# A two-layer sequence kernel: its background work ordered by an estimate of readiness, a product in column pairs, and masks moved to VectorE

## The chip, the cores and the metric

One core of a Trainium2 chip. The metric is device time of one execution in microseconds (us), the median of the runs. Engines are named TensorE (PE in the profile; PEld is its weight load), VectorE (DVE), ScalarE (ACT), GpSimd (POOL) and SyncE (SP), which issues the DMAs.

## The reference, cut to what is computed

```python
x = L0_attn_y_all                       # 4 sequences x 2048 tokens x 256
x = x + attn0(layernorm(x))             # one head, keys and values 64 wide, causal softmax
x = x + ffn0(layernorm(x))              # fp8-quantized input and weight, one 256x256 product
x = x + attn1(layernorm(x))             # 16 heads of 16, rotary positions, causal softmax
x = x + ffn1(layernorm(x))              # mix with the token before, sigmoid(r) * (relu(k)^2 @ Wv)
```

## The kernel before, in words

The work is cut into 16 chunks of 512 tokens: four sequences (b) of four chunks (qb). A chunk attends to its own and the earlier chunks of its sequence, so chunk qb has 4(qb+1) key tiles of 128.

**The main loop** is layer 1's attention. It runs over the chunks, in each over four groups of four heads (g), in each over the key tiles (kt): 640 steps. A step has

- the scores of four heads (`scores_of`, L640): for each head a product of 32 rows (16 key values and their rounding remainders) with the queries' high part, one with the low part, and one that adds the row shift; where the tile lies on the diagonal, four small bf16 products with `maskT_p` add minus infinity (L650). ScalarE takes the exponential (L657);
- the row maxima of four heads for a later group (`maxima_of`, L607): two products a head, on the diagonal four small products with `mask_p` (L615), then a VectorE maximum (L622). `all_maxima` fixes at which step each is due; near a change of chunk several fall into one step, and `whole_maxima` issues those beyond the first by themselves;
- the values of the step before (`weighted`, L680): four products of 32 columns each.

Scores and maxima use TensorE as four strips of 32 rows, so two score heads and two maxima heads share it: `together` issues pass by pass over the heads, first half of a step with score heads 0 and 1 and maxima heads 2 and 3, then the values, then the other half. The values use it as four strips of 32 columns. Every other product uses all 128 rows and columns.

**The background work** fills in between: generators of layer 0 for a chunk two or three ahead (list A: `a_in`, `a_mid`, `a_out`), layer 1's projections for the next chunk (Bq: `b_in`, `b_project`, `b_keys`, `b_queries`; Q: the second half of the queries) and the end of the chunk before (E: `end_half`). Each generator yields after a piece with its cost in us of TensorE time. At the end of every step `pull` takes pieces while the step's credit lasts. The credit is at least 1.75 us a step, more where a list must be done by a date (`rate_of`). A generator that yields a cost of 0 or more is not taken twice in one step; that, and a count of two steps in `b_keys`, is the only distance kept between a piece and what it waits for. `force` drains a list that is due.

**Layer 0** (`a_in`, `a_mid`, `a_out`): queries and keys are projected with the weights written twice, so that 128 rows hold the value twice (L327, 8 matmuls for half a chunk in the profile's records); the low parts are what rounding left (L334). `a_mid` takes the row maxima (L364, with a mask product L369 on the diagonal, maximum L370), then for each key tile the scores (L395 to L400), the exponential (L403) and the product with the values and a column of ones (L407), which adds up in one PSUM bank over the whole chunk: 65 columns, so that the row sum comes out beside the 64 values. `a_out` multiplies by the output weights (L429), whose 65th row is the bias, divides, and runs layer 0's feed-forward part.

**Buffers.** Seven PSUM banks are shared by all products, one more is layer 1's accumulator. `w2` is a pool of 13 buffers of 128 x 512; `live` counts those in use, and `full(n)` keeps two free. In each engine the program order is the order of issue. SyncE's queue has the loads, one x load a chunk (L109) and two output stores a chunk (L776).

Of the kernel before, what the change touches and what calls it, by code (L numbers as in the profile page):

```python
# [22 lines left out]
P = 128  # L23
# [11 lines left out]
NEG = -1e30  # L35


W2, PT = 13, 6
# [4 lines left out]
def seq_kernel(  # L43
# [26 lines left out]
    const = ctx.enter_context(tc.tile_pool(name="const", bufs=1))  # L70
    kv = ctx.enter_context(tc.tile_pool(name="kv", bufs=NB + 1))
# [13 lines left out]
    mask_b = const.tile([P, P], BF16, name="mask_b")  # L85
    make_causal_mask(nc, mask_b, mask_val=NEG)

# [28 lines left out]
    wqk0 = load_w(wqk0T, "wqk0", 4 * D0)  # L116
    wv0 = load_w(wv0T, "wv0", D0)
    bqk = const.tile([P, 2], F32, name="bqk")
# [4 lines left out]

    wo0 = const.tile([D0 + 1, C + 1], F32, name="wo0")
    nc.gpsimd.memset(wo0, 0.0)
    nc.gpsimd.memset(wo0[D0 : D0 + 1, C : C + 1], 1.0)
    nc.sync.dma_start(wo0[:D0, :C], wo0T)
    nc.sync.dma_start(wo0[D0 : D0 + 1, :C], bo0.rearrange("(o c) -> o c", o=1))
# [57 lines left out]
    for name, keep, fill, first, step in (  # L186
        ("ident_p", ALU.not_equal, 1.0, 1, -1),
        ("mask_p", ALU.is_ge, NEG, 1, -1),
        ("maskT_p", ALU.is_ge, NEG, -1, 1),
    ):  # L190
        t = const.tile([P, HG, P], BF16, name=name)
        nc.gpsimd.memset(t[:SLOT], 0.0)
        nc.gpsimd.affine_select(
            out=t[:SLOT], in_=t[:SLOT], pattern=[[first * SLOT, HG], [step, P]],
            compare_op=keep, fill=fill, base=0, channel_multiplier=first,
        )
        for h in range(1, HG):
            nc.sync.dma_start(t[h * SLOT : (h + 1) * SLOT], t[:SLOT])
        parts.append(t)
    ident_p, mask_p, maskT_p = parts  # L200
# [30 lines left out]
    HALF = BLK // 2  # L231

# [39 lines left out]
    def normal_T(x, out_to, hf, tag):  # L272

        my = stats(x, hf, tag)
        yield 0.0
        while full(2):
            yield None
        xn = w2n(f"xn_{tag}_{hf}")
        normalize(x, hf, my, xn)
        yield 0.0  # L280
        if not out_to:
            out_to.append(w2t(f"xT_{tag}_{hf}"))
        transpose(xn, out_to[0], f"{tag}_{hf}", nc.scalar.copy)
        done(1)
        yield 0.6
# [20 lines left out]
    def a_in(b, qb, x, hf):  # L306
# [6 lines left out]
        xT = to[0]  # L313
        if hf == 0:
            while full(2):
                yield None
            kT0[qb] = kv.tile([P, BLK], F32R, tag="kT0", name=f"kT_{tag}", bufs=NB)
            v0[qb] = kv.tile([P, TT, D0 + 1], F32, tag="v0", name=f"v_{tag}", bufs=NB)
            nc.gpsimd.memset(v0[qb][:, :, D0 : D0 + 1], 1.0)
            q0[b, qb] = w2(f"qh_{tag}", F32R), w2(f"ql_{tag}", F32R)  # L320
        kT, va, (qh, ql) = kT0[qb], v0[qb], q0[b, qb]
        flags.add((b, qb, "a", hf))
        cols = slice(hf * HALF, (hf + 1) * HALF)
        pq = bank(f"pq_{tag}_{hf}")
        for i in range(2):
            for k in range(CK):
                nc.tensor.matmul(  # L327
                    pq[:, i * HALF : (i + 1) * HALF], wqk0[:, k, i * P : (i + 1) * P],
                    xT[:, k, :], start=(k == 0), stop=(k == CK - 1),
                )  # L330
        for i, hi, lo, r in ((0, qh, ql, slice(0, P)), (1, kT, kT, slice(D0, P))):
            src = pq[:, i * HALF : (i + 1) * HALF]
            nc.scalar.activation(hi[:, cols], src, AF.Identity, bias=bqk[:, i : i + 1])
            nc.vector.scalar_tensor_tensor(  # L334
                lo[r, cols], src[r, :], bqk[r, i : i + 1], hi[r, cols].bitcast(F32),
                ALU.add, ALU.subtract,
            )
        yield -1.8
        pv = bank(f"pv_{tag}_{hf}")
        for j in range(2):  # L340
# [3 lines left out]
            va[:, 2 * hf : 2 * hf + 2, :D0],  # L344
# [4 lines left out]
        yield 0.9  # L349
        flags.add((b, qb, "in", hf))  # L350

    def a_mid(b, qb):
# [3 lines left out]
        qh, ql = q0.pop((b, qb))  # L356

        mx = small.tile([P, TT, NB], F32, tag="mx0", name=f"mx_{tag}")
        for t in range(TT):
            for kb in range(qb + 1):  # L360
                sc = bank(f"m_{tag}_{t}_{kb}")
                w = BLK if kb < qb else (t + 1) * P
                for q in (qh, ql):
                    nc.tensor.matmul(  # L364
                        sc[:, :w], q[:, t * P : (t + 1) * P], kT0[kb][:, :w],
                        start=(q is qh), stop=(kb < qb and q is ql),
                    )
                if kb == qb:
                    nc.tensor.matmul(sc[:, w - P : w], ident_b, mask_b, start=False, stop=True)  # L369
                nc.vector.reduce_max(mx[:, t, kb : kb + 1], sc[:, :w], axis=AX.X)  # L370
                if kb % 2 or kb == qb:
                    yield -0.6 * (1 + kb % 2)
# [3 lines left out]
        yield 0.0  # L376
        while full(3):
            yield None
        sh = w2(f"sh_{tag}", F32R)
        shift_rows(pads[2], sh, f"sh_{tag}")  # L380
        yield 0.5

        av = bank(f"av_{tag}")
        nkt = (qb + 1) * TT
        last = None
        for kt in range(nkt + 1):
            now = None
            if kt < nkt:
                while full(1):
                    yield None  # L390
                sc = bank(f"s_{tag}_{kt}")
                pT = w2(f"p_{tag}_{kt}")
                c0 = max(kt - qb * TT, 0) * P
                keys = kT0[kt // TT][:, (kt % TT) * P : (kt % TT + 1) * P]
                nc.tensor.matmul(sc[:, c0:], keys, qh[:, c0:], start=True, stop=False)  # L395
                nc.tensor.matmul(sc[:, c0:], keys, ql[:, c0:], start=False, stop=False)
                diag = kt >= qb * TT
                nc.tensor.matmul(sc[:, c0:], ones, sh[:, c0:], start=False, stop=not diag)
                if diag:
                    nc.tensor.matmul(  # L400
                        sc[:, c0 : c0 + P], ident_b, maskT_b, start=False, stop=True
                    )
                nc.scalar.activation(pT[:, c0:], sc[:, c0:], AF.Exp, scale=D0**-0.5)  # L403
                now = (kt, pT, c0)
            if last is not None:
                k, p, c = last
                nc.tensor.matmul(  # L407
                    av[: D0 + 1, c:], v0[k // TT][:, k % TT, :], p[:, c:],
                    start=(k == 0), stop=(k == nkt - 1),
                )  # L410
                done(1)
            last = now
            yield -1.7
        done(3)
        cx = w2(f"cx_{tag}")[: D0 + 1, :]
        nc.scalar.copy(cx, av[: D0 + 1, :])
        yield 0.0
        ctx0[b, qb] = cx

    def a_out(b, qb, x, hf):  # L420
# [4 lines left out]
        cx = ctx0[b, qb]  # L425
        t2 = slice(2 * hf, 2 * hf + 2)
        for t in range(2 * hf, 2 * hf + 2):
            o = bank(f"po_{tag}_{t}")
            nc.tensor.matmul(  # L429
                o[:, : C + 1], cx[:, t * P : (t + 1) * P], wo0, start=True, stop=True  # L430
            )
# [5 lines left out]
        if hf:  # L437
            done(1)
        my = stats(x, hf, f"f{tag}")
        yield 1.0  # L440
# [8 lines left out]
        yield 0.0  # L449
# [9 lines left out]
        yield 0.5  # L459
# [8 lines left out]
        yield 0.6  # L468
# [14 lines left out]
    def b_project(b, qb):  # L483

        tag = f"a1_{b}_{qb}"
        for t in range(TT):
            while (b, qb, t // 2) not in xT1 or full(2):
                yield None
            if t == 0:
# [25 lines left out]
            roped[b, qb, t] = count[0], qk, rb  # L515
            yield -1.8
# [8 lines left out]
            yield 0.9  # L525

    def b_keys(b, qb):

        tag = f"a1_{b}_{qb}"
        for t in range(TT):  # L530
            while (b, qb, t) not in roped or count[0] < roped[b, qb, t][0] + 2:
                yield None
            _, qk, kn = roped.pop((b, qb, t))
# [7 lines left out]
            yield 0.0  # L541
# [12 lines left out]
            yield -0.5  # L554

    def b_queries(b, qb, pair, hf):

        tag = f"a1_{b}_{qb}_{pair}"
        while (
            (b, qb, "k", 2 * hf + 1) not in flags or full(1)  # L560
            or (pair and order.index((b, qb)) > at[0] and at[1] < 2)
        ):
            yield None
        qd = w2(f"qd_{tag}_{hf}")
        src = qr1[b, qb][:, 2 * hf : 2 * hf + 2, pair * P : (pair + 1) * P]
# [6 lines left out]
        yield 0.0  # L572
# [7 lines left out]
        qh, ql = q1[b, qb, pair]  # L580
        pt = bank(f"pt_{tag}_{hf}")
# [11 lines left out]
        yield -0.5  # L593


    def maxima_of(b, qb, g, s, mx, heads):
# [3 lines left out]
        qs = [q[:, g % 2, :] for q in q1[b, qb, g // 2]]  # L600
        cols = slice(t * P, (t + 1) * P)
        w = BLK if kb < qb else (t + 1) * P
        scs = {h: bank(f"m_{b}_{qb}_{g}_{s}_{h}") for h in heads}

        def pass_(i, h):
            r = slice(h * SLOT, (h + 1) * SLOT)
            nc.tensor.matmul(  # L607
                scs[h][:, :w], qs[i][r, cols], kT1[b, kb][r, g, :w],
                start=(i == 0), stop=(kb < qb and i == 1),
            )  # L610

        def mask(v, h):
            if kb == qb:
                r = slice(h * SLOT, (h + 1) * SLOT)
                nc.tensor.matmul(  # L615
                    scs[h][:, w - P + v * SLOT : w], ident_p[r, v, :],
                    mask_p[r, v, v * SLOT :], start=False, stop=(v == HG - 1),
                )

        def drain():  # L620
            for h in heads:
                nc.vector.reduce_max(mx[:, t, h, kb : kb + 1], scs[h][:, :w], axis=AX.X)  # L622

        return heads, pass_, 2, mask, drain

    def scores_of(b, qb, g, kt, sh, heads):

        qs = [q[:, g % 2, :] for q in q1[b, qb, g // 2]]
        c0 = max(kt - qb * TT, 0) * P
        kcols = slice((kt % TT) * P, (kt % TT + 1) * P)  # L630
        diag = kt >= qb * TT
# [462 lines left out]
```

## Time and profile before

| | |
|---|---|
| runs | 3276.69, 3259.07, 3256.58 us; median 3259.07 |
| the profiled execution: its own time, its span | 3270.68 us, 3268.9 us |
| busy share: PE, PEld, DVE, ACT, POOL | 94%, 53%, 64%, 53%, 20% |
| mean granted TensorE clock | 0.955 |
| chain that ended last | PE 73%, DVE 18%, ACT 4%, issue 3%, POOL 2%, DMA 1% |
| idle time of TensorE, first matmul at | 182.5 us, 11.8 us |

The busy time of TensorE counts from a matmul's start to a modelled end, and matmuls overlap, so a busy PE is not PE at its peak. What a stretch of work costs TensorE is better read from the start of its first matmul to the start of the next stretch's first. A group's row gives instructions, busy time (overlaps counted once), mean duration of one, and the idle time of its engine just before, with what ended it. An fp32 product of 128x512 appears as two records.

### The profile page before, as it was taken

To read this page: it belongs to the slowest core of one execution; us is meant where nothing else is said; L and a number is where in the kernel's file an instruction comes from. 1 tells how busy PE (TensorE), PEld (TensorE's weight loads), DVE (VectorE), ACT (ScalarE), POOL (GpSimd) and SP (SyncE) were. 2 spreads that over 40 slices of the span, in tenths; PEclk is the share of its full clock that TensorE was granted. 3 is DMA by queue.
4 is the path that set the end of the run, shared out by engine and by line. 5 is a ranking of instruction groups with operands and counts; after the bars stand their busy time and mean duration, and the time that the engine had idled before them with its cause. 6 is when DMAs were issued, how large, how long until landed. Compare 5 with 4: busy or idle time off the path is not lost.

```text
span 3268.9 us, 75100 instructions
## 1 busy us (share of the span) xinstructions
PE 3086.4 (94%) x31392; PEld 1738.1 (53%) x31392; DVE 2080.0 (64%) x4408; ACT 1732.1 (53%) x3649; POOL 637.8 (20%) x991
## 2 busy tenths in 40 slices
PE   7889999999999999899999999989999999999988
PEld 4555555555556555545456555554545655554444
DVE  4556657676647676576745666667673677577771
ACT  2435455455555545546565454554655555555664
POOL 4312203121113301313003220122210421021000
PEclk8889899899999999989999899989999999999999
DMA  2000000000000000000000000000000000000000
GB/s 64 2 1 14 1 1 14 1 5 11 2 2 14 15 1 1 14 1 14 1 2 2 15 15 1 5 11 1 14 1 1 5 11 8 1 8 1 8 2 7
DMA packets 21045, 24.66 MB, mean 8 GB/s; under 512 B 1793, under 2 KB 20450, under 8 KB 20706
## 3 DMA queue, kind: packets, MB, share of 16 engines
q1 hardware_dynamic: 20706, 19.87, 1.9%
q8 instruction: 246, 4.03, 0.5%
q14 instruction: 93, 0.76, 0.1%
HBM read 11.18 MB, written 8.39 MB: 6 GB/s over the span
## 4 chain that ended last, share of the span: by engine, by line
PE 73%; DVE 18%; ACT 4%; issue 3%; POOL 2%; DMA 1%; POOLq 0%; ACTq 0%; DVEq 0%
PE s L640 19%; PE av L680 15%; DVE mx L622 10%; PE m L607 8%; PE av_a L407 4%; PE pq_a L267 3%; PE s L650 2%; PE pk_f L751 2%; PE po_f L267 2%; PE m_a L364 2%; PE m L615 2%; PE pr_f L267 1%; PE pw_f L267 1%; PE pv_a L267 1%; PE s_a L395 1%
## 5 line engine op out<-in xcount | busy, mean ns | idle before, releaser
L622 DVE TENSOR_REDUCE mx<-m 128x1 f32<-128x512 f32 (+3 forms) x2560 | 1423.8, 604 | 721.7 <-PE m L607 331.5
L657 ACT ACTIVATE p<-s 128x512 f32<-128x512 f32 (+3 forms) x2560 | 1224.5, 532 | 1189.7 <-PE s L640 626.7
L607 PE MATMUL m<-kT_a,qh_a 32*128 32x512 f32 (+3 forms) x2560 | 735.5, 471 | 78.8 <-DVE mx L622 41.3
L680 PE MATMUL av<-p,v_a 128*32 128x512 f32 (+3 forms) x5120 | 642.0, 560 | 0.1
L640 PE MATMUL s<-qh_a,kT_a 32*128 32x512 f32 (+3 forms) x2560 | 622.3, 466 | 15.8 <-DVE mx L622 14.0
L640 PEld LDWEIGHTS s<-qh_a,kT_a 32*128 32x128 f32 x2560 | 255.1, 186 | 705.9 <-issue 285.6
L607 PE MATMUL m<-kT_a,ql_a 32*128 32x512 f32 (+3 forms) x2560 | 561.8, 392 | 0.0
L640 PE MATMUL s<-ql_a,kT_a 32*128 32x512 f32 (+3 forms) x2560 | 510.1, 396 | 0.0
L640 PE MATMUL s<-sh,ones 32*128 32x512 f32 (+3 forms) x2560 | 478.8, 370 | 0.0
L607 PEld LDWEIGHTS m<-kT_a,qh_a 32*128 32x128 f32 x2560 | 314.8, 189 | 206.2 <-DVE mx L622 127.2
L607 PEld LDWEIGHTS m<-kT_a,ql_a 32*128 32x128 f32 x2560 | 276.4, 192 | 0.0
L640 PEld LDWEIGHTS s<-sh,ones 32*128 32x128 f32 x2560 | 248.5, 190 | 24.3 <-ACT sh L301 2.3
L640 PEld LDWEIGHTS s<-ql_a,kT_a 32*128 32x128 f32 x2560 | 246.1, 189 | 0.0
L241 POOL TENSOR_SCALAR v_f<-mv_f 128x2 f32<-128x2 f32 x32 | 7.0, 219 | 964.1 <-DVE mv_f L239 963.6
L615 PE MATMUL m<-mask_p,ident_p 32*128 32x96 bf16 (+3 forms) x4096 | 194.5, 203 | 0.0
L680 PEld LDWEIGHTS av<-p,v_a 128*32 128x32 f32 x5120 | 107.8, 109 | 156.2 <-issue 121.3
L650 PE MATMUL s<-maskT_p,ident_p 32*128 32x32 bf16 (+3 forms) x4096 | 172.5, 198 | 0.0
L407 PE MATMUL av_a<-p_a,v_a 128*65 128x512 f32 (+3 forms) x320 | 145.5, 536 | 2.8 <-ACT p_a L403 1.6
L615 PEld LDWEIGHTS <-ident_p 32*128 32x128 bf16 x4096 | 135.5, 97 | 3.8 <-issue 0.6
L267 PE MATMUL pq_a<-wqkv,xT_a 128*128 128x512 f32 x256 | 128.8, 627 | 0.0
L650 PEld LDWEIGHTS <-ident_p 32*128 32x128 bf16 x4096 | 90.0, 93 | 47.9 <-issue 35.5
L241 POOL TENSOR_SCALAR v_a<-mv_a 128x2 f32<-128x2 f32 x64 | 14.1, 221 | 461.7 <-DVE mv_a L239 460.9
(160 smaller groups left out, 3847.3 us busy)
## 6 DMA issues: line engine op xcount, KB each, us to landing
x<-in_x SPq DMA_DIRECT2D x16, 512.0 KB, 4.1
out_y<-x SPq DMA_DIRECT2D x32, 256.0 KB, 2.1
wqkv<-in_wqkv1T SPq DMA_DIRECT2D x1, 768.0 KB, 9.2
wqk<-in_wqk0T SPq DMA_DIRECT2D x1, 256.0 KB, 4.3
wc<-in_wfT SPq DMA_DIRECT2D x1, 256.0 KB, 7.6
wo<-in_wo1T SPq DMA_DIRECT2D x1, 256.0 KB, 5.1
wr<-in_wrT SPq DMA_DIRECT2D x1, 256.0 KB, 5.0
wk<-in_wkT SPq DMA_DIRECT2D x1, 256.0 KB, 5.0
```

The lines of the kernel that those rows point to most:

```text
L267: nc.tensor.matmul(dst, lhsT[:, k, t * P : (t + 1) * P], w[:, k, :], start=(k == 0), stop=(k == CK - 1),)
L364: nc.tensor.matmul(sc[:, :w], q[:, t * P : (t + 1) * P], kT0[kb][:, :w], start=(q is qh), stop=(kb < qb and q is ql),)
L395: nc.tensor.matmul(sc[:, c0:], keys, qh[:, c0:], start=True, stop=False)
L407: nc.tensor.matmul(av[: D0 + 1, c:], v0[k // TT][:, k % TT, :], p[:, c:], start=(k == 0), stop=(k == nkt - 1),)
L607: nc.tensor.matmul(scs[h][:, :w], qs[i][r, cols], kT1[b, kb][r, g, :w], start=(i == 0), stop=(kb < qb and i == 1),)
L615: nc.tensor.matmul(scs[h][:, w - P + v * SLOT : w], ident_p[r, v, :], mask_p[r, v, v * SLOT :], start=False, stop=(v == HG - 1),)
L622: nc.vector.reduce_max(mx[:, t, h, kb : kb + 1], scs[h][:, :w], axis=AX.X)
L640: nc.tensor.matmul(scs[h][:, c0:], ones[r, :] if i == 2 else kT1[b, kt // TT][r, g, kcols], sh[r, c0:] if i == 2 else qs[i][r, c0:], start ...
L650: nc.tensor.matmul(scs[h][:, c0 : c0 + (v + 1) * SLOT], ident_p[r, v, :], maskT_p[r, v, : (v + 1) * SLOT], start=False, stop=(v == HG - 1),)
L657: nc.scalar.activation(pTs[h][:, c0:], scs[h][:, c0:], AF.Exp, scale=DK**-0.5)
L680: nc.tensor.matmul(av[h * SLOT : (h + 1) * SLOT, c0:], v1[b, kt // TT][:, kt % TT, at : at + SLOT], pTs[h][:, c0:], start=(kt == 0), stop= ...
L751: nc.tensor.matmul(pk[:, d * HALF : (d + 1) * HALF], wk[:, k, d * P : (d + 1) * P], xk[:, k, :], start=(k == 0), stop=(k == CK - 1),)
```

## The change

Five edits go together.

1. **The order of the background work.** A class `Clock` follows the instructions as they are issued and keeps, with fixed costs, when each engine would be free and when each operand would be written. A generator now yields before a piece: its cost, the `w2` buffers that it needs, and the operands that it reads. `pull` takes a piece only if the latest of these is no more than 150 ns after TensorE's place on that clock; `pull_first` (in `force`, in the start-up and ahead of a chunk's `cn`) takes the one that would be ready first. The two-step count in `b_keys` and the once-a-step rule are gone. The credit is no longer at least 1.75 us a step: it is `min(1.75, spare work / steps left in the chunk)`.
2. **Layer 0's values.** `narrow_values` handles two key tiles at once: four products of 32 columns (two tiles, two halves of the 64 values) into the four strips of a fresh bank. ScalarE copies the bank out, GpSimd adds it to `cx` and adds the two exponentials to `sums`; the output weights stand twice above each other (`wo0` is 128 rows), so their product adds the two tiles' strips, and a product with a column of ones gives the row sum. The bias is added to x by GpSimd in `a_in`. A pair is taken right behind layer 1's `weighted` when its exponentials are there.
3. **Layer 0's queries and keys** are projected once (128 columns for both together), rounded once, and written twice by six DMAs a chunk on SyncE's queue.
4. **The maxima's masks** on the diagonal, in both layers, are no longer products: `row_max` has VectorE add a mask tile and take the maximum in one `tensor_tensor_reduce`.
5. `together` goes over the four heads in turn, each head's exponential or maximum issued right behind its last product; in the second half of a step the maxima heads come first. `w2` has 12 buffers.

```diff
+    def row_max(dst, sc, w, diag):
+        if diag:
+            trash = small.tile([P, BLK], BF16, tag="trash", name="trash", bufs=1)
+            nc.vector.tensor_tensor_reduce(
+                trash[:, :w], sc[:, :w], mask_w[:, BLK - w :], 1.0, LOWEST, ALU.add, ALU.max, dst
+            )
+        else:
+            nc.vector.reduce_max(dst, sc[:, :w], axis=AX.X)
...
-        pq = bank(f"pq_{tag}_{hf}")
-        for i in range(2):
-            for k in range(CK):
-                nc.tensor.matmul(
-                    pq[:, i * HALF : (i + 1) * HALF], wqk0[:, k, i * P : (i + 1) * P],
-                    xT[:, k, :], start=(k == 0), stop=(k == CK - 1),
-                )
...
+        pq = bank(f"pq_{tag}_{hf}")[:, :HALF]
+        for k in range(CK):
+            nc.tensor.matmul(pq, wqk0[:, k, :], xT[:, k, :], start=(k == 0), stop=(k == CK - 1))
...
+        if hf:
+            for dst, src in (
+                (qh[:D0], th[:D0]), (qh[D0:], th[:D0]), (kT[:D0], th[D0:]),
+                (ql[:D0], tl[:D0]), (ql[D0:], tl[:D0]), (kT[D0:], tl[D0:]),
+            ):
+                nc.sync.dma_start(dst.bitcast(F32), src.bitcast(F32))
...
-                nc.tensor.matmul(
-                    av[: D0 + 1, c:], v0[k // TT][:, k % TT, :], p[:, c:],
-                    start=(k == 0), stop=(k == nkt - 1),
-                )
...
+    def narrow_values():
+        b, qb, kt, c0, pTs, cx, sums = narrow.pop(0)
+        tag = f"a0_{b}_{qb}_{kt}"
+        av = bank(f"av_{tag}")
+        for z in range(4):
+            j, d = divmod(z, 2)
+            nc.tensor.matmul(
+                av[z * SLOT : (z + 1) * SLOT, c0:],
+                v0[kt // TT][:, kt % TT + j, d * SLOT : (d + 1) * SLOT], pTs[j][:, c0:],
+                start=True, stop=True,
+            )
+        if kt == 0:
+            nc.scalar.copy(cx, av)
+            nc.gpsimd.tensor_tensor(sums, pTs[0], pTs[1], ALU.add)
+        else:
+            part = w2(f"avs_{tag}")
+            nc.scalar.copy(part[:, c0:], av[:, c0:])
+            for add, to in ((part, cx), (pTs[0], sums), (pTs[1], sums)):
+                nc.gpsimd.tensor_tensor(to[:, c0:], to[:, c0:], add[:, c0:], ALU.add)
+            done(1)
+        done(2)
+        flags.add((b, qb, "ctx", kt))
...
-        def mask(v, h):
-            if kb == qb:
-                r = slice(h * SLOT, (h + 1) * SLOT)
-                nc.tensor.matmul(
-                    scs[h][:, w - P + v * SLOT : w], ident_p[r, v, :],
-                    mask_p[r, v, v * SLOT :], start=False, stop=(v == HG - 1),
-                )
...
+    def pull(lists, floor):
+        some, moved = False, True
+        while moved:
+            moved = False
             for gens in lists:
                 for gen in list(gens):
...
+                    t = start_of(gens, gen)
+                    if t is None or t > clock.pe + SLACK:
                         continue
...
+                    if asked[id(gen)][0] and credit <= floor:
                         continue
...
+                    emit(gens, gen)
                     moved = some = True
...
-        rate = BASE
+        spare = sum(loads[id(z)][0] for z in (A, Bq, Q, E)) + sum(
+            a_work(*order[j]) for j in range(a_next, min(i + 4, N))
+        )
+        rate = min(BASE, spare / to(4))
...
             if last is not None:
                 weighted(*last)
+                clock.follow()
+                if narrow and clock.when(*narrow[0][4]) < clock.pe + SLACK:
+                    narrow_values()
```

## The prediction

> **What bounds the kernel now.** I read the page first: the busy shares, the clock row, the chain.
>
> ```profile
> PE 3086.4 (94%) x31392; PEld 1738.1 (53%) x31392; DVE 2080.0 (64%) x4408; ACT 1732.1 (53%) x3649; POOL 637.8 (20%) x991
> ...
> PEclk8889899899999999989999899989999999999999
> ...
> PE 73%; DVE 18%; ACT 4%; issue 3%; POOL 2%; DMA 1%; POOLq 0%; ACTq 0%; DVEq 0%
> ```
>
> TensorE is the bound, VectorE the second link (18% of the chain). The clock is mostly full; at its mean of 0.955 it costs (1 - 0.955) x 3269 = 147 us. Then TensorE's timeline in one step, at full clock: is the half step with mask products longer?
>
> ```profile
> 1122.76 0.49 PE L640 MATMUL s<-qh_a,kT_a 32*128 32x512 f32 x2
> 1122.76 0.50 PE L607 MATMUL m<-kT_a,qh_a 32*128 32x512 f32 x2
> ...
> 1123.32 0.40 PE L640 MATMUL s<-sh,ones 32*128 32x512 f32 x2
> 1123.65 0.66 PE L546 MATMUL pk_a<-ident,rb_a 128*128 128x128 f32 x4
> 1124.14 1.03 PE L267 MATMUL pv_a<-wqkv,xT_a 128*128 128x256 f32 x4
> 1125.10 0.49 PE L640 MATMUL s<-qh_a,kT_a 32*128 32x512 f32 x2
> ...
> 1125.45 0.32 PE L615 MATMUL m<-mask_p,ident_p 32*128 32x128 bf16 x8
> 1125.67 0.39 PE L640 MATMUL s<-sh,ones 32*128 32x512 f32 x2
> 1125.99 0.64 PE L680 MATMUL av<-p,v_a 128*32 128x512 f32 x4
> ```
>
> It is not. The half without masks runs from 1122.76 to 1123.65, the half with eight from 1125.10 to 1125.99: both 0.89 us. The masks run in the maxima's strips while the scores' third pass runs in theirs.
>
> I then cut the trace at layer 1's value products (steps at full clock only) and took off each step's 128-row work. A step with one set of maxima takes 2.79 us (median) when it has over 1 us of such work, but 3.44 us (mean of 132) when it has less; with two sets 4.3 to 4.7 us. So where background work is thin, a step is set by the release of PSUM banks by VectorE (four maxima at 684 ns are 2.7 us) and ScalarE, not by TensorE. The waits of TensorE say what the rest stalls on:
>
> ```profile
> PE m L607 <- DVE mx L622: 41.3, 119, 2.3
> PE pt_a L584 <- POOL qd_a L567: 19.3, 5, 4.7
> PE pk_a L546 <- DVE rb_a L537: 19.1, 14, 1.8
> ```
>
> The last two are background pieces taken before their operands were there. All such pieces (pt_a, pk_a, pt_f, pt_sh, ptf_a) cost 73 us of idle TensorE, 12 of them before the first matmul.
>
> **What the Trainium skill says.** "TensorE: Matmul & The Clock Gate", Part 1: the clock drops to half after an idle window of some 3.4 us. The trace agrees in kind: only 1.0 and 0.5 occur, and a half-speed stretch follows the first steps of a chunk, where maxima pile up (4.77 us for one run of them at 1153 us). "TensorEngine Tiling (Array Packing)", Key Properties: changing the tiling mode drains TensorE. The trace agrees: three passes of 0.22 us take 0.89 us, about 0.2 us more. "VectorE: DVE Perf Modes", Two Vector instructions with no wait between them: an operation with an accumulator output is two instructions. Before has none, but the built order of after has 1088 such pairs.
>
> **The change part by part**, against the profiled span of 3269 us.
>
> *Layer 0's values.* From each run of L407 to TensorE's next instruction adds up to 128 us for 160 products. After: 80 pairs. A set of four 32-column products of layer 1 takes 1.00 us with its mode change, so they overlap, and 0.86 us without. 64 full pairs x 0.86 + 16 half ones x 0.43 = 62 us; in the order of after nearly all stand right behind layer 1's values, so there is no new mode change. -66 us, less 4 for 64 one-column products: **-62**.
>
> *Queries and keys.* 64 of 128 products of 256 columns go; eight records (four products) in a row take 1.89 us including the mode change, 0.43 us each without. **-27**.
>
> *Masks.* Layer 0: 64 products at some 0.08 us, **-5**. Layer 1: nothing beside a third pass or the scores' own masks; only where scores are 256 wide and maxima 512 does the half fall from 0.83 to 0.75 us (94 cases): **-7**. Cover gone would mean whole sets issued alone, but these wait for VectorE anyway.
>
> *Mode changes*, counted in both orders: 2337 before, 2305 after. 32 x 0.2 = **-7**.
>
> *VectorE.* 1088 maxima become sum-and-maximum. Nearest rows:
>
> ```profile
> L622 DVE TENSOR_REDUCE mx<-m 128x1 f32<-128x512 f32 x1792 | 1140.7, 684 | 413.3 <-PE m L607 331.5 <-PE s L640 49.9 <-PE m L615 28.7
> L717 DVE TENSOR_TENSOR x<-po_f,x 128x512 f32<-128x512 f32 x32 | 22.1, 692 | 40.4 <-PE po_f L267 40.4
> L741 DVE SCALAR_TENSOR_TENSOR mix_f<-xs_f,mu_sb,mix_f 128x256 f32<-128x256 f32 x128 | 71.0, 615 | 35.2 <-ACT mix_f L738 35.2
> L434 DVE SCALAR_TENSOR_TENSOR x<-po_a,rs_a,x 128x256 f32<-128x256 f32 x64 | 31.0, 484 | 2.3
> L239 DVE BATCH_NORM_AGGREGATE mv_a<-st_a 128x2 f32<-128x6 f32 x128 | 23.3, 182 | 4.4
> ```
>
> With one operand in PSUM a two-operand pass takes 692 ns against 684. The accumulator read is not in the trace: at most 182 ns like the tiny rows, at least some 50; I take 100, as it has no input. The second of two also waits for the first (they share `trash`), some 20 ns on average. So +0.12 us each, 130 us of VectorE's time (70 to 230), less 16 for a rounding pass that goes. Most lies under TensorE. Queued behind are the next maxima and hence PSUM banks. It shows where background work is thin, about a quarter of the diagonal sets: 64 x 4 x 0.12 = **+30** (15 to 60).
>
> *Thinner steps.* The order of after has 309 steps with under 1 us of 128-row work, before 270. 39 x 0.65 x 0.75 (three in four have maxima) = **+19**.
>
> *Order by readiness.* It removes part of the 61 us of late operands after the start; it can't move the maxima, and its clock counts neither the reuse of `w2` buffers nor PSUM banks when it decides. I take half, **-30** (0 to -61), and **-15** of the clock's 147 us (+30 to -73).
>
> *GpSimd, ScalarE, SyncE.* GpSimd gets 192 sums 512 wide at 1.29 us and 48 at 0.74 us: 289 us, 20% to 29% busy. ScalarE gets 64 copies at 0.59 us, loses 32 at 0.48 us: +23 us. SyncE issues 96 more DMAs at some 0.45 us; the last of six lands 6 x 0.45 + 2.3 us = 5 us after the rounding (the SBUF to SBUF copy of `ident_p` took 2.3 us to land). They queue behind output stores, which wait for GpSimd. All are hidden by the two or three chunks by which layer 0 runs ahead: **0** (to +80, below). Only the first chunk pays the 5 us, and it has fewer pieces ahead of it.
>
> Sum: -62 -27 -5 -7 -7 +30 +19 -30 -15 = -104. The span becomes 3165 us, the execution 3167 us. The profiled execution (3270.68) is 11.6 us above the median of 3259.07, so on that scale 3167 x 3259.07 / 3270.68 = 3155 us.
>
> **Rivals.**
>
> *The order gains more.* All 61 us of late operands go (-31 more), half of the half-clock loss (-58), and thin steps cost nothing (-19): 3155 - 108 = 3047 us. For it: half clock follows stalls. Against: the largest stalls are VectorE's maxima, whose steps are the same.
>
> *A new wait eats it.* A layer-0 exponential's buffer is now held until GpSimd's three sums are done, 3.9 us a pair where steps of about 5 us take one pair, beside 4.3 us of rotary work for each tile of the next chunk. If GpSimd falls behind, ScalarE waits for a `w2` buffer in front of layer 1's exponentials, then TensorE for banks. 5 us in each of 16 chunks: +80, 3235 us. Against: GpSimd is 20% busy, and two buffers stay free.
>
> *VectorE becomes the bound; slower.* If the new pass runs at half rate, as L741 does with two SBUF operands (615 against 484 ns shows part of it), and the read and wait take 0.26 us, a full set takes 4 x (0.69 + 0.53 + 0.26) = 5.9 us, with other VectorE work (656 us over 640 steps) 6.9, against about 4.9 us for a mean step: 64 x 2.0 = 128. A set 384 wide gives 5.8, 64 x 0.9 = 58, narrower ones some 15. 3155 - 30 + 200 = 3325 us. It decides above about 0.45 us of extra a maximum, where the full sets alone eat the gain. Against: one operand is in PSUM, as in L434.
>
> *It doesn't do what it says*: the pairs don't overlap. Layer 1's do; I give it nothing apart.
>
> **Chances.** As forecast 0.50 (3100 to 3210), more from the order 0.25, a new wait 0.19, VectorE the bound 0.06. Under 1% a measurement here can't tell from no change, so faster means under 3226 us: the first two and 0.08 of the third, 0.83; the rest of the third, 0.11, is the same; slower 0.06. The range 3050 to 3240 leaves out the slow case, and the edges of the second and third.
>
> **What would show it.** L615 gone with half steps still at 0.89 us; the new L388 at some 690 ns (512 wide) and 50 to 180 for its read; the value pairs at 0.9 us; VectorE's idle before maxima smaller; waits of pt_a and pk_a near zero. Wrong if half steps get shorter, if GpSimd's sums or SyncE's copies head TensorE's waits, or if the mean clock moves by over 0.02.

## The result, and the profile after

The changed kernel takes 3237.07 us (median of 6 runs, 3232.41 to 3238.71) against 3266.48 us for the kernel before (6 runs): a ratio of 0.9909, interval 0.9887 to 0.9931. The profiled execution took 3235.0 us, its span is 3233.2 us against 3268.9, so 36 us were gained where the sum of the prediction had 104. It is 0.9% of the time, just under the 1% from which the prediction counted a gain as faster. The page of the changed kernel, busy shares, clock and chain:

```profile
PE 3032.2 (94%) x27552; PEld 1676.7 (52%) x27552; DVE 2098.3 (65%) x5464; ACT 1754.8 (54%) x3681; POOL 915.5 (28%) x1245
...
PEclk9869899989999999999999999999999999999999
...
PE 72%; DVE 20%; issue 3%; POOL 2%; ACT 2%; DMA 0%; SPq 0%; DVEq 0%; POOLq 0%; ACTq 0%
```

TensorE has 54 us less of busy time and is still the bound. The clock row has one new low digit, the 6, in the third slice (162 to 243 us, chunk (0,0) and the start of (0,1)); later there are more nines than before. The mean clock is 0.956 after 0.955.

TensorE's timeline in a step of chunk (1,2):

```profile
1242.67 0.49 PE L798 MATMUL s<-qh_a,kT_a 32*128 32x512 f32 x2
1242.67 0.51 PE L781 MATMUL m<-kT_a,qh_a 32*128 32x512 f32 x2
...
1243.24 0.39 PE L798 MATMUL s<-sh,ones 32*128 32x512 f32 x2
1243.56 1.07 PE L833 MATMUL av<-p,v_a 128*32 128x512 f32 x8
1244.44 1.04 PE L580 MATMUL av_a<-p_a,v_a 128*32 128x512 f32 x8
1245.41 0.50 PE L781 MATMUL m<-kT_a,qh_a 32*128 32x512 f32 x2
```

The half step takes 0.89 us (1242.67 to 1243.56), as before. Layer 0's new pair (L580) stands behind layer 1's values (L833); its four products overlap. The two together take 1.85 us (1243.56 to 1245.41, also the median of 81 cases at full clock), where layer 1's values alone take 1.00 us (median of 531): the mode change behind them only moves behind the pair, and a pair adds 0.85 us.

The waits of TensorE (us in total, times, longest):

```profile
PE pt_a L422 <- DVE xn_a L411: 25.0, 4, 11.5
...
PE pk_a L724 <- DVE rb_a L715: 12.8, 8, 3.8
PE pt_sh L457 <- DVE pad L450: 11.9, 16, 2.5
...
PE pt_a L762 <- POOL qd_a L745: 6.3, 3, 2.6
```

The first of these was, in the kernel before:

```profile
PE pt_a L261 <- DVE xn_a L250: 13.5, 2, 11.8
```

Late operands did not get fewer in sum; they moved. pt_a for qd_a fell from 19.3 to 6.3 us and pk_a for rb_a from 19.1 to 12.8, but pt_a for xn_a rose from 13.5 to 25.0 and pt_sh for `pad` from 3.8 to 11.9. All waits of pt_a, pk_a, pt_f, pt_sh, pt_sh_a and ptf_a for their operands add up to 63 us before and 74 after: 26 and 17 us behind chunk (0,1), but 37 and 57 in the start and the first two chunks. The masked maximum on VectorE:

```profile
L388 DVE CUSTOM_DVE_ANT_0 trash<-m,mask_w 128x512 bf16<-128x512 f32 x256 | 176.7, 690 | 92.7 <-PE m L781 54.2 <-PE s L808 10.5 <-DVE mx L388 1.0
...
L388 DVE DVE_READ_ACCUMULATOR2_ANT mx<- 128x1 f32 x1024 | 84.9, 83 | 0.1
```

690 ns for 512 columns and 83 ns for the read; the forecast had 692 and 100. VectorE's idle time before layer 1's maxima fell from 721.7 us to 331.4 + 341.7 = 673.1.

**Where the time went** shows when the span is cut at the first value product of each chunk of layer 1. Sequences 1 and 2 gained what such a sum promises (3%): sequence 1 takes 774.2 us after 798.7, sequence 2 772.1 after 798.6. Sequence 3, in which layer 0 has the least left to do (17 of the 160 value products of the kernel before fall into it, 40 into sequence 1), gained only 4.8 us. Of sequence 0 the chunks (0,2) and (0,3) fell by 13.7 us. The start and the first two chunks lost it: they end at 440.5 us, before at 406.6. The windows of the kernel before (stretch, its length, then busy time and instructions of PE, PEld, DVE, ACT, POOL, granted clock, DMA share, GB/s), the start first, then chunks (0,0) and (0,1):

```profile
0.00:114.30 114.30, 83.11 (x498) 58.25 (x498) 50.58 (x145) 30.96 (x60) 44.61 (x88) 0.83 0.15 46
114.30:218.30 104.00, 92.32 (x1127) 60.45 (x1123) 61.37 (x149) 44.05 (x105) 30.12 (x44) 0.81 0.01 2
218.30:406.60 188.30, 178.04 (x1799) 105.30 (x1799) 124.61 (x270) 93.27 (x200) 39.22 (x60) 0.95 0.03 7
```

and of the changed kernel:

```profile
0.00:109.60 109.60, 64.04 (x298) 42.56 (x299) 41.22 (x142) 23.79 (x45) 49.81 (x90) 0.83 0.18 55
109.60:238.50 128.90, 109.10 (x966) 67.69 (x967) 71.22 (x229) 51.47 (x117) 45.73 (x61) 0.78 0.03 7
238.50:440.50 202.00, 188.21 (x1598) 109.31 (x1598) 133.60 (x344) 95.24 (x203) 61.83 (x80) 0.91 0.05 14
```

The start lasts nearly as long with a quarter less work on TensorE (64 us busy, not 83), and that work turns up in (0,0): 25 us longer, at a clock of 0.78. In the order of issue, the kernel before has layer 0 of chunk (0,1) through its maxima, its scores and its output product when layer 1's first maximum comes; the changed kernel has one half of its projections. A line of the start-up, `keep[id(A2)] = 7`, lets that chunk take a piece only while 7 of the 12 `w2` buffers stay free (elsewhere 2).

### The profile page after: what moved, and what is told of

It is laid out like the page before. It is cut to its first block, busy times and chain, and to the rows that moved or that the text cites. A ratio compares the mean times of both kernels' runs of the same rounds, so it can differ in the third digit from the quotient of the medians.

```text
span 3233.2 us, 70078 instructions
## 1 busy us (share of the span) xinstructions
PE 3032.2 (94%) x27552; PEld 1676.7 (52%) x27552; DVE 2098.3 (65%) x5464; ACT 1754.8 (54%) x3681; POOL 915.5 (28%) x1245
## 4 chain that ended last, share of the span: by engine, by line
PE 72%; DVE 20%; issue 3%; POOL 2%; ACT 2%; DMA 0%; SPq 0%; DVEq 0%; POOLq 0%; ACTq 0%
PE s L798 16%; PE av L833 15%; PE m L781 12%; DVE mx L392 8%; DVE trash L388 5%; PE pq_a L428 3%; PE pv_a L428 2%; PE av_a L580 2%; PE s L808 2%; PE pk_f L903 2%; PE pr_f L428 2%; PE po_f L428 2%; PE m_a L528 2%; PE s_a L549 1%; PE pw_f L428 1%
## 5 line engine op out<-in xcount | busy, mean ns | idle before, releaser
L392 DVE TENSOR_REDUCE mx<-m 128x1 f32<-128x512 f32 x1536 | 978.1, 684 | 331.4 <-PE m L781 323.4
L781 PE MATMUL m<-kT_a,qh_a 32*128 32x512 f32 (+3 forms) x2560 | 709.2, 469 | 49.6 <-DVE mx L392 31.2
L388 DVE CUSTOM_DVE_ANT_0 trash<-m,mask_w 128x128 bf16<-128x128 f32 (+3 forms) x1024 | 501.5, 490 | 341.7 <-PE m L781 235.2
L798 PE MATMUL s<-qh_a,kT_a 32*128 32x512 f32 (+3 forms) x2560 | 653.9, 464 | 44.4 <-DVE mx L392 19.9
L833 PE MATMUL av<-p,v_a 128*32 128x512 f32 (+3 forms) x5120 | 649.3, 557 | 0.1
L798 PE MATMUL s<-ql_a,kT_a 32*128 32x512 f32 (+3 forms) x2560 | 533.9, 391 | 0.0
L833 PEld LDWEIGHTS av<-p,v_a 128*32 128x32 f32 x5120 | 112.2, 109 | 183.0 <-issue 141.0
L808 PE MATMUL s<-maskT_p,ident_p 32*128 32x64 bf16 (+3 forms) x4096 | 183.2, 198 | 0.0
L592 POOL TENSOR_TENSOR sum_a<-sum_a,p_a 128x512 f32<-128x512 f32 (+1 forms) x128 | 146.5, 1144 | 5.0
L925 POOL TENSOR_TENSOR x<-x,sg_f 128x512 f32<-128x512 f32 x32 | 41.1, 1286 | 320.6 <-DVE sg_f L924 319.6
L592 POOL TENSOR_TENSOR cx_a<-cx_a,avs_a 128x512 f32<-128x512 f32 (+1 forms) x64 | 73.2, 1144 | 204.8 <-ACT avs_a L590 204.8
L808 PEld LDWEIGHTS <-ident_p 32*128 32x128 bf16 x4096 | 99.6, 93 | 57.1 <-issue 49.9
```

Source lines behind the costliest of these rows:

```text
L388: nc.vector.tensor_tensor_reduce(trash[:, :w], sc[:, :w], mask_w[:, BLK - w :], 1.0, LOWEST, ALU.add, ALU.max, dst)
L392: nc.vector.reduce_max(dst, sc[:, :w], axis=AX.X)
L592: nc.gpsimd.tensor_tensor(to[:, c0:], to[:, c0:], add[:, c0:], ALU.add)
L781: nc.tensor.matmul(sc[:, :w], q1[b, qb, g // 2][i][r, g % 2, t * P : (t + 1) * P], kT1[b, kb][r, g, :w], start=(i == 0), stop=(i == 1),)
L798: nc.tensor.matmul(sc[:, c0:], ones[r, :] if i == 2 else keys, sh[r, c0:] if i == 2 else q1[b, qb, g // 2][i][r, g % 2, c0:], start=(i == ...
L808: nc.tensor.matmul(sc[:, c0 : c0 + (v + 1) * SLOT], ident_p[r, v, :], maskT_p[r, v, : (v + 1) * SLOT], start=False, stop=(v == HG - 1),)
```

## The experiments

Theory 1: holding layer 0 of chunk (0,1) back in the start is what is lost. Theory 2, the rival: VectorE's masked maxima eat the gain. The prediction's rival, a wait through GpSimd's sums, comes third. Each ratio is to the kernel before.

**start_keep4**: the line is eased, so that layer 0 of that chunk goes ahead of layer 1's first maximum, all but a part of its feed-forward.

```diff
-    keep[id(A2)] = 7
+    keep[id(A2)] = 4
```

> The changed kernel with one number changed: in the start-up, layer 0 of the second chunk must leave 4 work buffers free instead of 7, so that all of it may be issued before the main loop. Theory 1 (the start eats the gain: layer 0 of the second chunk is held back, and chunks (0,0) and (0,1) then run half empty at half clock): the main loop starts later than at 110 us, but chunk (0,0) falls from 129 to some 95 us, and the whole is 25 to 40 us below the changed kernel (3237), 3197 to 3212. Theory 2 (VectorE's new work eats the gain everywhere): nothing moves, 3227 to 3247.

3188.84 us, ratio 0.9779 (0.9747 to 0.9811): 48 us less than the changed kernel. The start is 18.5 us longer, (0,0) 44.2 us shorter, (0,1) 22.8 shorter; no other chunk moved by more than 4.3. Its windows of (0,0) and (0,1):

```profile
128.10:212.70 84.60, 81.87 (x862) 48.91 (x860) 60.16 (x197) 41.70 (x101) 27.02 (x39) 0.92 0.05 11
212.70:391.90 179.20, 170.89 (x1565) 98.51 (x1564) 128.63 (x330) 94.25 (x201) 60.62 (x79) 0.96 0.04 12
```

The waits within (0,0), first of the changed kernel (its three longest), then of this one, from the top of its list:

```profile
PE ptf_a L632 <- POOL q_a L623: 4.6, 1, 4.6
PE pk_a L724 <- DVE rb_a L715: 3.6, 2, 2.9
PE pt_a L422 <- DVE xn_a L411: 3.6, 1, 3.6
```
```profile
PE m L781 <- DVE mx L392: 0.7, 3, 0.3
PE pt_a L422 <- DVE xn_a L411: 0.5, 1, 0.5
```

Three single stalls of 3 to 5 us are gone, and half-clock time with them: in (0,0) 57.2 us at half clock become 13.0, in (0,1) 34.4 become 14.6. In the changed kernel one half-clock stretch (14 us) begins right at the end of the 4.6 us stall, one (20 us) within the last of the three; a third, of 24 us, begins without any stall over 0.8 us ahead of it, so the stalls are not all of it. More was won than theory 1 had put down.

**before_hold**, the same from the other side: the kernel *before*, with that chunk held back.

```diff
-        pull([A2], -2.5)
+        if count[0] < 6:
+            pull([A2], -2.5)
```

> The kernel before with one edit: from the sixth round of its start on, layer 0 of chunk (0,1) gets no more pieces, so that before the first maximum of layer 1 only one half of it is projected, as in the changed kernel (before: 20 maxima products, 28 score records and half of the output product too). Theory 1 (the start is the failed step, apart from everything else in the change): chunk (0,0) gets longer by 20 to 40 us with more half-clock time there, (0,1) by 5 to 25, the time before the first values shorter by 5 to 20, the rest within 5; ratio to before 1.006 to 1.016. Theory 2 (the two first chunks lose to something else in the change, like the waits for GpSimd or for the doubled keys): ratio 0.997 to 1.003.

3290.26 us, ratio 1.0083 (1.0058 to 1.0109). The windows of (0,0) and (0,1):

```profile
104.50:236.50 132.00, 114.42 (x1178) 73.28 (x1176) 67.32 (x169) 49.83 (x115) 32.14 (x48) 0.78 0.00 1
236.50:439.00 202.50, 188.85 (x1833) 113.29 (x1832) 128.69 (x279) 93.77 (x201) 39.16 (x60) 0.94 0.02 7
```

(0,0) is 28.0 us longer and (0,1) 14.2, against 24.9 and 13.7 in the changed kernel, at the same clock of 0.78 in (0,0). (The trace of the kernel before has the whole output product of that chunk ahead, 8 records of L429, and not half of it.) Here too a single stall comes up in (0,0), of 7.4 us, where the kernel before has one of 4.7. The start alone, without any other part of the change, makes the same loss: start and first two chunks get 32 us longer, in the changed kernel 34. Theory 1 holds from both sides.

**after_nomask, after_pemask, before_nomask** ask for theory 2. The first leaves the masks of the maxima out of the changed kernel (maxima over all columns, exponentials with a hundredth of their scale), the second puts them back on TensorE, the third leaves the mask products out of the kernel before (again with a hundredth of the scale).

```diff
 after_nomask
-        if diag:
+        if False:
 after_pemask: row_max is reduce_max alone, and
+        if kb == qb:
+            for v in range(HG):
+                nc.tensor.matmul(sc[:, w - P + v * SLOT : w], ident_p[r, v, :],
+                    mask_p[r, v, v * SLOT :], start=False, stop=(v == HG - 1))
 before_nomask: L369 gone, and at L613
-            if kb == qb:
+            if False:
```

> The changed kernel without any mask in the maxima (both layers): plain VectorE maxima; and the exponentials' scale is a hundredth, so that nothing overflows. It leaves out the mask of the maxima. Theory 1: only the accumulator reads and the waits on the scratch tile go, 10 to 30 us less than the changed kernel, 3207 to 3227. Theory 2: 70 us or more less, at most 3167.

> The changed kernel with the maxima's masks back on TensorE as small bf16 products, in both layers; all else as changed. Theory 1: TensorE gets some 12 us back and VectorE loses 90 us of which little is on the path: 3215 to 3245, the same as the changed kernel within 1%. Theory 2: clearly faster than the changed kernel, at most 3195. A third way, that the products' issue cost TensorE more than the half steps show: slower, above 3260.

> The kernel before without the maxima's mask products in both layers, and with the exponentials' scale a hundredth. It leaves out the mask of the maxima. The prediction's step (the products hide beside the scores' third pass, -12 us): 0.994 to 0.998 of before. The rival that the products cost TensorE a share of their 210 us of busy time: 0.975 or less.

Measured: 3169.86 us, 0.9714 (0.9689 to 0.974); 3209.48, 0.9841 (0.9812 to 0.9871); 3244.11, 0.9965 (0.9941 to 0.9989). The first is beyond theory 1's number and nearly at theory 2's: masks on VectorE cost the changed kernel some 64 to 67 us. But the gain over the second, which has the masks on TensorE, is only 3237 - 3209 = 28 us (22 by the ratios). So masks cost some 40 us as products in the new order, where they cost 0.0035 x 3259 = 11 us (4 to 19) in the old one. In the new order both prices were wrong and their difference about right: forecast +30 - 12 = +18, measured +22 to +28. Half of both is clock: from the changed kernel to after_nomask the span falls by 71 us and half-clock time by 69, which is worth 35; from after_pemask to after_nomask it is 43 us and 39, worth 19. Without masks the loss of the start stays: (0,0) is only some 6 us shorter. Theory 2 has a part in the miss, of 10 us or less. Why the products cost more in the new order was not settled; the new order issues the maxima heads first in the second half of a step.

**after_cost, keep4_cost**: is the estimate too cheap for the masked maximum? The class `Clock` is given its measured time.

```diff
+            if "ISA" in kind or "Custom" in kind:
+                return 155 + 1.045 * n if n > 1 else 83
```

> The changed kernel, but its clock is told what a masked maximum takes (155 + 1.045 ns a column, 83 ns for the read, as the trace of the changed kernel has them) instead of a flat 200 ns for each of the two. Theory A (the masked maxima cost by their own VectorE time, which no order can hide): within 12 us of the changed kernel's 3237. Theory B (they cost because the order by readiness believes VectorE free too early): 15 to 45 us less, 3192 to 3222.

> The changed kernel with the start-up's 4 free buffers and the right cost of the masked maxima together. Theory A: as with the 4 buffers alone, 3180 to 3198. Theory B: 15 to 45 us less than that, 3144 to 3174.

3225.7 us, 0.9874 (0.9847 to 0.9902), and 3181.75, 0.975 (0.9722 to 0.9777): 11 and 7 us less than without the edit. Both are what theory A put down, and the intervals overlap with those without the edit: the cheap estimate explains little of what the masks cost.

**after_slack**: `pull` takes a piece whose operands come up to 2 us later, not 0.15.

```diff
-                    if t is None or t > clock.pe + SLACK:
+                    if t is None or t > clock.pe + 2000:
```

> The changed kernel, but pieces are taken when the estimate says that their operands are there within 2000 ns, instead of 150. If taking pieces by readiness is worth the 30 us that the prediction gave it, waits of pt_a, pk_a, pt_f for their operands come back: 3255 to 3290. If it is worth nothing (the pieces of the kernel before were rarely late after the start): 3225 to 3250.

3513.78 us, 1.0752 (1.0708 to 1.0796), far outside both. The waits that head TensorE's list:

```profile
PE pk_a L724 <- DVE rb_a L715: 48.7, 24, 3.6
PE pt_a L422 <- DVE xn_a L411: 36.6, 14, 11.7
```

Pieces are taken ahead of their operands throughout, and the clock falls to 0.922. The changed kernel has no other distance left between a piece and what it waits for, so the test carries all of it. That is its worth within the new kernel, not against the spacing of the old one.

**keep4_pemask**: both edits that gained.

> The changed kernel with the start-up's 4 free buffers and with the maxima's masks back on TensorE. If the two effects add (-48 and -28 us): 3150 to 3172. If the gain from the masks on TensorE lay in the start (a different start-up order) and not in the steady chunks: 3180 to 3198.

3158.4 us, 0.9677 (0.965 to 0.9704), clock 0.971. The two gains add up (48 + 28 of 3237 would give 3161). This version beats both kernels.

**pemask_rate**: that version with the old credit, at least 1.75 us a step.

```diff
-        rate = min(BASE, spare / to(4))
+        rate = BASE
```

> Against keep4_pemask (3158.4 us, ratio 0.968): one more edit, the credit of a step is at least 1.75 us again, as in the kernel before, and not the share of the spare work. The prediction's term 'thinner steps' (+19) says that evening the work out is the cost: with the old credit the work comes in earlier steps and 5 to 15 us come back, ratio 0.963 to 0.966. If the readiness test sets where the pieces go and the credit seldom does: within 4 us, ratio 0.966 to 0.970. If spreading the work is what keeps the late steps full: 5 to 20 us more.

3207.86 us, 0.9833 (0.9795 to 0.987): 49 us more, beyond all three. (0,0) loses 11 us and the chunks (1,1), (2,1), (3,1) 13 to 18 each; half-clock time goes from 185 to 257 us, which is worth 36 of the 44 us between the two spans. In this version spreading the work evenly is a gain of the change and not a price. Why the old credit brings the half clock was not shown.

**keep4_nosum**: start_keep4 without the one-column products; the reciprocal is taken of another column.

```diff
-            nc.tensor.matmul(o[:, C : C + 1], sums[:, cols], one, start=True, stop=True)
-            nc.vector.reciprocal(rs, o[:, C : C + 1])
+            nc.vector.reciprocal(rs, o[:, C - 1 : C])
```

> Against start_keep4 (3188.8 us, ratio 0.978): leaves out the 64 one-column products that give layer 0's row sums; the reciprocal is taken of a column of the output product, so that the values are other ones. If each of these products costs TensorE a whole weight load, as the class of output products says (30 us before, 50.5 after), 12 to 22 us less: ratio 0.9715 to 0.9745. If they cost the 4 us that the prediction gave them: ratio 0.976 to 0.978.

3170.66 us, 0.9721 (0.97 to 0.9742): 18 us less than start_keep4 (the spans 14), as was put down for a whole weight load each. But the gain is not spread as these products are, four for each chunk of layer 0: (1,1), (2,1) and (3,1) fall by 7 to 10 us each, as they do in keep4_cost, which still has the products, and all else together gets 10 us longer. Safer is TensorE's own time: the stretches from the start of a run of output and row-sum products to the next product add up to 44.7 us in start_keep4 and to 32.5 here, 12 us for the 64. The changed kernel's timeline shows one such product:

```profile
1267.03 0.59 PE L608 MATMUL po_a<-wo,cx_a 128*128 128x256 f32 x2
1267.46 0.28 PE L609 MATMUL po_a<-one,sum_a 128*128 128x1 f32 x2
1267.67 0.39 PE L798 MATMUL s<-qh_a,kT_a 32*128 32x256 f32 x2
```

256 columns take 0.43 us from start to next start, one column takes 0.21, with the mode change behind it; where no mode change follows it is 0.14.

**keep4_nopool**: start_keep4 with GpSimd's two sums of exponentials left out after a chunk's first pair (layer 0's exponential with a hundredth of its scale).

```diff
-            for add, to in ((part, cx), (pTs[0], sums), (pTs[1], sums)):
+            for add, to in ((part, cx),):
```

> Against start_keep4 (ratio 0.978): GpSimd's two sums of exponentials a pair are left out after a chunk's first pair (layer 0's exponential gets a hundredth of its scale to stay finite; the row sums are other ones), so that a pair's exponentials come free some 2.6 us earlier and GpSimd loses about 150 us of work. Rival 'a new wait eats it' (buffers held by GpSimd's sums): 25 to 80 us less, ratio 0.953 to 0.970. If GpSimd is hidden, as the prediction's step says: within 8 us, ratio 0.9755 to 0.980.

3198.97 us, 0.9808 (0.9783 to 0.9833), 10 us *more* than with the sums. GpSimd lost 144 us of busy time and nothing came of it: all of the span but (0,0) is 8 us shorter, and (0,0) is 21 us longer, with 43 us at half clock after 13. The rival of a wait through GpSimd's two sums of exponentials is out. The run also shows how much the first chunk depends on small shifts of the order: of the 48 us of start_keep4, some 10 to 20 may be such luck, though keep4_cost and keep4_pemask, with shifts of their own, kept a gain of 44 to 51 us over their partners.

## Why the prediction was wrong

The range (3050 to 3240) held the time by 3 us, and the likeliest case (3155) missed it by 82 us. That the rival *a new wait eats it* stood at 3235 us is luck: keep4_nopool finds nothing of its wait. TensorE stayed the bound, and the parts were the right ones. One step failed, the start, and one term was mis-sized, the row sums. Term by term, in us of span:

| step | forecast | the runs |
|---|---|---|
| layer 0's values | -66 | -54 on TensorE (128 to 74); about -64 as an estimate, since 0.12 us of mode change is moved 81 times from layer 1's values to the pairs |
| row sums | +4 | +14 to +20: output and row-sum products 30 to 44.7 (start_keep4) or 50.5 (changed kernel), 12 of it the row sums |
| queries and keys | -27 | -29: 63 to 34 on TensorE |
| masks to VectorE (+30 -5 -7) | +18 | +22 to +28 (after_pemask) |
| start, layer 0 of chunk (0,1) held back | 0 | +28 (before_hold) to +48 (start_keep4) |
| mode changes, order, clock, thinner steps (-7 -30 -15 +19) | -33 | not measured by themselves; some -7 to -39 are left of the measured -36 |

**The failed step** is the one that gave the start nothing: "Only the first chunk pays the 5 us, and it has fewer pieces ahead of it." Its first half held: TensorE waits once, in the start, for a doubled key, 3.7 us. Its second half was taken for harmless, and the sum has no term for the start. Fewer pieces ahead mean that they come later, into the 16 steps of chunk (0,0), at whose end layer 1 needs them. Single waits of 3 to 5 us come up there, and TensorE goes to half clock: of the 25 us that (0,0) gets longer, 8 are idle time of TensorE, up to 9 are the loss by 18 us more of half clock, and the rest is work that came later. Before_hold makes this loss in the old kernel (+28 and +14 us in the first two chunks), start_keep4 takes it out of the new one. The orders of issue showed it beforehand: the sum took mode changes and thin steps from them, and not what stands ahead of the first step.

**Sizes.** The row-sum products were mis-sized, 4 us for 64 of them where they take some 12 of TensorE's time: one column was taken as cheap because it streams little. That is 0.19 us each, about the length of one weight load of 128x128 (L609, 195 ns on average, one for each of the two records); that the load is the cause was not tested. The value pair was sized rightly (0.86 forecast, 0.85 measured). Masks: both halves too small in the new order, 30 for 64 and 12 for 40, but 12 was right in the old one (11). GpSimd's sums were put at 289 us; the prediction's own counts give 283, and its busy time rose by 278.

**Order by readiness and clock** (-30 and -15). The 61 us from which half was taken hold some 10 us of waits for VectorE's maxima (pt_f for L622, 7.5 us, the largest), which are not late operands. Behind chunk (0,1) late operands fell by 9 us; in the start and the first two chunks they rose by 20. So the test is needed in the new kernel, which has given up every other spacing (after_slack, +277 us), but what it gained in late operands over the old spacing is small. The clock went the same two ways: half-clock time fell from 200 to 155 us behind (0,1), worth 23, and rose from 97 to 130 us up to its end.

**Thinner steps** (+19). The steps with under 1 us of 128-row work did rise by about as many as forecast, 39: counted in the traces, from one value product to the next, they are 197 before and 235 after. Their price stays unmeasured. The credit does not set their number (226 in keep4_pemask, 230 in pemask_rate), so the 49 us of pemask_rate are no answer on this term.

**Right**: the half steps at 0.89 us with and without masks beside the third pass; the maximum's 690 ns and its read of 83; queries and keys; GpSimd's sums hidden (keep4_nopool), SyncE's copies hidden but for the one wait of 3.7 us; VectorE not the bound. The waits of pt_a and pk_a did not go "near zero": those for qd_a and rb_a halved, from 38.4 to 19.1 us, and pt_a's for xn_a rose by 11.5.

## What to carry to other kernels

In a software pipeline, cost the fill by itself: list what stands ahead of the first steady step in both orders, since every piece missing there returns in steps that have no cover. Take the price of a product of one column from a trace: here it was about 0.2 us, near half of that of 256 columns. When a term is the difference of two hidden costs, the difference may be right while both are wrong; run one side alone before building on either. And see where a gain falls before giving it to an edit: 10 us can come from half-clock stretches that a small shift of the order moves.

## What the runs showed of the hardware

- The masked maximum takes 690, 556, 423 and 290 ns for 512, 384, 256 and 128 columns. The Trainium skill, "VectorE: DVE Perf Modes", The TRN2 errata, gives an fp32 tensor_tensor as (N+151)/0.96 ns: 691, 557, 424, 291. The trace agrees within 2 ns for layer 1's 1024, also with one operand in PSUM and a maximum carried along (layer 0's 64 take 682 to 284 ns, 6 to 8 less); the accumulator's read (83 ns) comes on top.
- Half-clock stretches come in pieces of one length: of the 35 in the changed kernel's trace 34 are whole multiples of 3.41 us (14 of them one piece, 7 two, 6 three), and a chunk's total is often 3.4, 6.8, 10.2 or 17.1 us. The Trainium skill, "TensorE: Matmul & The Clock Gate", Part 1, names a window of some 3.4 us, and these lengths agree. So a stall costs more than itself where it drops a whole window to half speed, and a small shift of the order can move it: chunk (1,1) takes 162.0 us with 10.2 at half clock in the changed kernel and in start_keep4, and 154.8 us with none in after_cost, keep4_cost and keep4_nosum.
